# Four modulated convolution layers: two single-bank tiles for the last accumulator, and two steps moved in early iterations

## The chip, the cores and the metric

The kernel runs on one core of a Trainium2 chip. The metric is the time of one execution on the device in microseconds; the median of several executions is compared. The core has a matrix engine (TensorE, PE in the profile, with PEld for its weight loads), a vector engine (VectorE, DVE), a scalar engine (ScalarE, ACT), GpSimd (POOL) and a queue processor (SyncE, SP), which issues most of the DMA transfers. Each works through its own queue in order, and they meet at semaphores. Products land in PSUM, in banks of 512 float32 numbers for each of 128 partitions.

## The reference

`x` is 128 x 64 x 1024 in float32 (samples, channels, positions), `style` 128 x 128.

```python
def _layer(x, style, w, b, mw, mb, typ):
    s = style @ mw.T + mb
    weight = SCALE * w * s[:, None, :, None]
    demod = lax.rsqrt(jnp.sum(weight * weight, axis=(2, 3)) + EPS)
    weight = weight * demod[:, :, None, None]
    if typ == 'same':
        out = jax.vmap(_conv_same)(x, weight) + b[None, :, None]
    elif typ == 'upsample':
        out = jax.vmap(_conv_up)(x, weight.transpose(0, 2, 1, 3)) + b[None, :, None]
        out = _blur(out, 2.0 * blur_k, (1, 1))
    elif typ == 'downsample':
        xb = _blur(x, blur_k, (2, 2))
        out = jax.vmap(_conv_down)(xb, weight) + b[None, :, None]
    return out
...
out = x
for i, typ in enumerate(('same', 'upsample', 'same', 'downsample')):
    out = _layer(out, style, weights[i], biases[i], mod_w[i], mod_b[i], typ)
return x + out
```

Every sample has its own weights of three taps, scaled by its style. There is no nonlinearity between the layers, so for one sample the four layers are one linear map of the signal plus a constant.

## The kernel before, in words

The kernel works on that linear map. For each sample it multiplies the four layers' weights (and the blur) into one filter of nine taps of 64 x 64, and then convolves the signal once with it. The constants that the biases leave in each row, and the few positions at both ends of the signal, are computed apart.

Four samples make a **quad**; there are 32 quads (`NQ`). A quad's work is in two parts.

*Weights.* `scale3` scales layer 3's weights (ScalarE). `stage1` multiplies them by layer 2's into the PSUM tiles psS, and ScalarE evicts them as S. From quad 7 on this is done in two halves: `stage1_a` makes the first products and ScalarE evicts them (line 361); `stage1_b` adds further products to the same banks and VectorE evicts those (line 443). `stage2` multiplies S by the blur and layer 1 (E) into psR, evicted as R, and `stage3` (or `stage3_b` and `stage3_a`) by layer 0 into psW or a free accumulator, evicted as Wf. `combine_a` and `combine_b` (VectorE) form sums H of the nine taps. All PSUM tiles psS, psR and psW come from one pool, `ps_w`, with two tiles of one bank each and one buffer: whoever takes them next waits until the last reader has let go.

*Signal.* The signal lies in three interleaved planes. VectorE and GpSimd make differences of the planes (G and T). The convolution is done in five products instead of nine taps: `conv3`, `conv1`, `conv2`, `conv4` and `conv0`, each of three groups of four matmul instructions, which alternate between two banks: bank s takes the channel rows of half s. `conv3` opens the accumulator psA of the quad; `copy_m3` copies it to SBUF (ScalarE, line 793); `conv1` adds to it; `sum1` forms y (VectorE, line 663); `conv2` adds again; `sum2` forms Y, a second accumulator of two banks that all quads share, and finishes y (line 813); `conv4` adds to Y and `conv0` to psA. `outputs(q, i)` evicts plane i on ScalarE, two banks in turn (`output`, line 831; plane 0 from psA, 1 from y, 2 from Y), and stores each plane. psA comes from the pool `ps_conv`, with two buffers of two banks, each one tile.

The order of the instructions on each engine is the order in which the code is written. One pass of `turn_of(q)` does, mixed with each other, the end of quad q, the signal of n = q + 1, stages 2 and 3 of c = q + 2 and stage 1 of s = q + 4. Iterations 0 to 3 are a variant, `early_turn`; iteration 4 (`entry`) is the first of `turn_of`, with some steps of its own. Behind iteration 28 the last three quads are written out by hand.

Two details matter here. First, in iterations 1 to 6 (`SMALL`) the row constants of the later samples are computed by a pair of small matmuls into spare columns of Y's second bank: VectorE clears these columns with a memset, `small(q)` multiplies into them (line 1238), and VectorE reads them in the next iteration (`small_rest`). Second, waits are found by tile: an instruction that uses a tile waits for the readers or writers of any part of that tile that the framework counts as overlapping, and PSUM accesses of two engines to one tile are put one after another.

Of the kernel before, what the change touches and what calls it, by code (L numbers as in the profile page):

```python
# [55 lines left out]
K = 3  # L56
# [7 lines left out]
def kernel(  # L64
# [12 lines left out]
    NQ = B // 4  # L77
# [20 lines left out]
    ps_w = ctx.enter_context(tc.tile_pool(name="ps_w", bufs=1, space=PSUM))  # L98
# [65 lines left out]
    def unit(pool, name):  # L164

        if pool is ps_w:
            return [pool.tile([P, 512], F32, tag=f"u{r}", name=f"{name}_{r}") for r in range(2)]
        t = pool.tile([P, 2, 512], F32, tag="u", name=name)
        return [t[:, r, :] for r in range(2)]
# [189 lines left out]
    def scaled_copy(eng, dst, src, f):  # L359
        if eng is nc_a:  # L360
            nc_a.activation(dst, src, AF.Copy, scale=f)  # L361
        else:
            eng.tensor_scalar(dst, src, f, None, op0=ALU.mult)
# [23 lines left out]
    def tap_matmul(ps, wd, at, n, weight, taps, first=False, last=False):  # L387
        for r, rows in enumerate(HALF):
            for c, cols in enumerate(HALF):
                nc.tensor.matmul(  # L390
                    ps[r][cols, at * C : (at + n) * C],
                    weight[rows],
                    wd[c if r == 0 else 1 - c][rows, taps],
                    start=first,
                    stop=last,
                    skip_group_check=True,
                )

    def s_tiles(q):
        t = s_pool.tile([P, 2, 8, C], F32, tag="S", name=f"S{q}")  # L400
        return [t[:, r] for r in range(2)], t

    def flat(t):
        return t.rearrange("c a o -> c (a o)")
# [18 lines left out]
    def stage1_a(q, ps=None):  # L423

        ps = ps or unit(ps_w, f"psS{q}")
        wd = chain[q]
        tap_matmul(ps, wd, 2, 2, w2n[:, 0, :], EVEN, first=True)
        tap_matmul(ps, wd, 3, 2, w2n[:, 2, :], EVEN)
        tap_matmul(ps, wd, 1, 1, w2n[:, 1, :], slice(1, 2))
        st, t = s_tiles(q)  # L430
        for r in range(2):
            scaled_copy(nc_a, flat(st[r][:, :4]), ps[r][:, C : 5 * C], tBn[:, q, r : r + 1])
        chain[q] = wd, ps, st, t
# [309 lines left out]
    def product(q, m, ps, groups=range(K)):  # L743

        W, H_ = Wq[q]
        tag, i = SLOT[m]
        for g in groups:
            for s, rows in enumerate(HALF):
                for c, cols in enumerate(HALF):
                    if m in (0, 4):  # L750
                        w = W[rows, tap(m // 2, g), c, :]
                    else:
                        w = H_[rows, m - 1, g, c, :]
                    nc.tensor.matmul(  # L754
                        ps[s][cols, :NB],
                        w,
                        Ts[q, tag][rows, c, i, g : g + NB],
                        start=(g == 0 and m == 3),
                        stop=(g == K - 1),
                        skip_group_check=True,  # L760
                    )

    def m_tile(tag, q, bufs=1):
        return mpool.tile([P, 2, NB], F32, tag=tag, name=f"{tag}_{q}", bufs=bufs)
# [3 lines left out]
    def parts(q):  # L768

        if isinstance(A[q], list):  # L770
            return [(slice(s, s + 1), A[q][s][:, None, :NB]) for s in range(2)]
        return [(slice(0, 2), A[q][:, :, :NB])]

    def banks(q):
        return A[q] if isinstance(A[q], list) else [A[q][:, s] for s in range(2)]
# [3 lines left out]
    def open_a(q):  # L779
        A[q] = ps_conv.tile([P, 2, 512], F32, tag="u", name=f"psA{q}")  # L780
        return banks(q)

    def conv3(q, pool=None):
        if pool:
            A[q] = unit(pool, f"psA{q}")
        elif q not in A:
            open_a(q)
        product(q, 3, banks(q))

    def copy_m3(q):  # L790
        m3c[q] = m_tile("m3", q)
        for s, a in parts(q):
            nc_a.copy(m3c[q][:, s], a)

    def conv1(q, *groups):
        product(q, 1, banks(q), groups or range(K))
# [7 lines left out]
    def conv2(q, *groups):  # L804
        product(q, 2, banks(q), groups or range(K))

    def sum2(q, steps=(0, 1)):
        if 0 in steps:
            m3 = m3c.pop(q)
            for s, a in enumerate(banks(q)):  # L810
                sum_of(Y[:, s, :NB], m3[:, s], 3.0, a[:, :NB])
        for s, a in parts(q) if 1 in steps else ():
            nc_v.tensor_sub(y1w[q][:, s], y1w[q][:, s], a)  # L813

    def conv4(q, *groups):
        product(q, 4, Y_banks, groups or range(K))
# [6 lines left out]
    def output(q, i, s, eng=nc_a):  # L823

        if q not in os:
            os[q] = opool.tile([P, 2, K, NB], F32, tag="o", name=f"o{q}")
        d3, add = td[:, q, s : s + 1], tb[:, q, s : s + 1]
        src = (banks(q)[s][:, :NB], y1w[q][:, s], Y[:, s, :NB])[i]
        dst = os[q][:, s, i]
        if eng is nc_a:  # L830
            nc_a.activation(dst, src, AF.Identity, bias=add, scale=d3)  # L831
        else:
            eng.tensor_scalar(dst, src, d3, add, op0=ALU.mult, op1=ALU.add)

    def store(q, s, planes=slice(0, K), queue=nc.sync):
        queue.dma_start(
            out[q, :, s, planes.start * NB : planes.stop * NB],
            os[q][:, s, planes].rearrange("c i j -> c (i j)"),
        )
# [11 lines left out]
    def last(i, n, j):  # L851
        ps, w = ends_ps[0]
        return ps[i][:, : n * w].rearrange("c (b j) -> c b j", b=n)[:, :, :j]
# [105 lines left out]
    def spread(t, n):  # L959

        return t[:, :, None].to_broadcast([P, t.shape[1], n])
# [132 lines left out]
    def rest3():  # L1094
        for h in range(2):
            bs = slice(h * HB, (h + 1) * HB)
            nc_v.scalar_tensor_tensor(
                Oe[:, bs],
                last(h, HB, 3),
                0.125,  # L1100
                spread(dm[:, 3, bs], 3),
                op0=ALU.mult,
                op1=ALU.mult,
            )
# [204 lines left out]
    def late(q):  # L1309
        return AHEAD <= q < NQ - 2  # L1310

    def outputs(q, i):
        for r in range(2):
            output(q, i, r)
            if late(q):
                store(q, r, slice(i, i + 1))
# [96 lines left out]
    def turn_of(q):  # L1413
        n, c, s = q + 1, q + 2, q + 4
        entry = q == FIRST
        stage2(c)
        if entry:
            sum2(q)
            conv4(q)
            combine_a(n)  # L1420
            r_sums(c, nc_v)
        else:
            conv2(q)
            r_sums(c, nc_g)
            sum2(q)
            in2(n, nc_g)
        side(TABLES, q)
        for i in range(3):
            load(c + 1, slice(i, i + 1))
        stage3_b(c, open_a(n))  # L1430
        if entry:
            conv0(q, 0, 1)
        else:
            combine_a(n)
            conv4(q)
        stage3_a(c)
        combine_b(n)
        conv3(n)
        if entry:
            copy_m3(n)  # L1440
        outputs(q, 2)
        if s < NQ:
            stage1_a(s)
        if not entry:
            copy_m3(n)
        in04(n)
        if sharing(q):
            share_sums(c + 1)
        in_g2(c)
        side(SIDE, q)  # L1450
        if q in SMALL:
            l, bs = SMALL[q]
            nc_v.memset(high(bs.stop - bs.start), 0.0)
        conv0(q, *((2,) if entry else range(K)))
        if entry:
            conv1(n, 0, 1)
        outputs(q, 1)
        if s < NQ:
            stage1_b(s)
        in_g01(c)  # L1460
        if sharing(q):
            share(c + 1, banks(q))
            share_copy(c + 1)
        outputs(q, 0)
        if q in SLOTS:
            matmuls, width, rest = SLOTS[q]
            slot(matmuls, width, Y_banks)
            rest()
        if s == NQ:
            slot(ends3, 3, unit(ps_w, "psE"), 3)  # L1470
            rest3()
        if q in SMALL:
            small(q)
        conv1(n, *((2,) if entry else range(K)))
        sum1(n)
        in3(c)
        side(LATE, q)
        if s == NQ:
            in04(c)
        in1(c, nc_g)  # L1480
        if s + 1 < NQ:
            scale3(s + 1)
# [6 lines left out]
    q, n, c = NQ - 3, NQ - 2, NQ - 1  # L1489
# [30 lines left out]
    in2(c, nc_v)  # L1520

    q, n = NQ - 2, NQ - 1
    conv3(n)
    copy_m3(n)
    conv4(q, 0, 1)
    for i in range(2):
# [109 lines left out]
```

## Time and profile before

| what | value |
|---|---|
| median of three runs | 479.57 us (479.07 to 479.76) |
| profiled execution: time / span | 480.28 us / 478.5 us |
| TensorE busy | 470.0 us, 98% |
| VectorE busy | 417.8 us, 87% |
| ScalarE busy | 310.1 us, 65% |
| GpSimd busy | 162.6 us, 34% |
| moved by DMA | 70.70 MB, 148 GB/s on the mean |
| granted TensorE clock | 0.997 |

The span runs from the first to the last instruction of the profiled execution; its time has 1.8 us more around it. In a row of the timeline the first number is the start, the second the length of a merged group, then engine, line, operation, tiles (out<-in), the shape and the count; in brackets stands the idle time of the engine ahead of it and what ended it. A row of a weight load (PEld) shows best where TensorE had to wait.

### The profile page before, as it was taken

The numbers are of one execution on the slowest core, as the hardware profiler recorded it, in microseconds if no ns is written. First come the engines' busy times: TensorE is split into PE (matmuls) and PEld (weight loads), VectorE is DVE, ScalarE is ACT, GpSimd is POOL, SyncE is SP. The second block draws the span as 40 slices with busy tenths as digits, with TensorE's granted clock in tenths as the row PEclk, the third lists the DMA queues.
The fourth block names the chain that finished last, engine by engine and source line by source line (L and its number), as shares of the span: only waits on it lengthen the run. The fifth ranks groups of instructions, "written<-read, shape, count | busy, mean of one in ns | idle before, by whom it ended". The sixth has DMA issues, their size and how long they took to land.

```text
span 478.5 us, 26719 instructions
## 1 busy us (share of the span) xinstructions
PE 470.0 (98%) x11928; PEld 348.4 (73%) x11928; DVE 417.8 (87%) x689; ACT 310.1 (65%) x708; POOL 162.6 (34%) x197
## 2 busy tenths in 40 slices
PE   8999999999999999999999999999999999999995
PEld 7877797777778876677776677767898777766652
DVE  5789998879889899899979899979989999999895
ACT  5465657577766676766667666667666767766352
POOL 2434033664435342243432233422333432333200
PEclk9999999999999999999999999999999999999998
DMA  7115356444455554355553455534555554445125
GB/s 234 58 68 182 130 184 204 149 121 154 147 150 150 180 156 144 121 150 159 171 160 118 123 170 152 179 122 126 144 164 166 165 149 148 149 146 174 61 91 191
DMA packets 50514, 70.70 MB, mean 148 GB/s; under 512 B 5664, under 2 KB 47328, under 8 KB 50400
## 3 DMA queue, kind: packets, MB, share of 16 engines
q1 hardware_dynamic: 49808, 68.32, 45.8%
q8 instruction: 93, 1.52, 1.5%
q10 hardware_dynamic: 592, 0.69, 0.5%
q14 instruction: 21, 0.17, 0.1%
HBM read 35.36 MB, written 33.62 MB: 144 GB/s over the span
## 4 chain that ended last, share of the span: by engine, by line
PE 95%; DVE 2%; DMA 1%; issue 0%; ACT 0%; SPq 0%; ACTq 0%
PE psA L754 45%; PE Y L754 11%; PE psR L468 9%; PE psA L572 7%; PE psW L572 7%; PE psS L390 6%; PE psR L534 4%; PE psA L468 2%; PE Y L995 2%; DMA par_s<-in_params_s 1%; DVE H L663 1%; PE Y L337 1%; DVE G L663 0%; PE psM L205 0%; ACT o L831 0%
## 5 line engine op out<-in xcount | busy, mean ns | idle before, releaser
L754 PE MATMUL psA<-T,H 64*64 64x340 f32 x2304 | 186.6, 447 | 0.4 <-DVE y L663 0.2
L754 PEld LDWEIGHTS psA<-T,H 64*64 64x64 f32 x2304 | 90.9, 133 | 48.1 <-issue 2.6
L663 DVE SCALAR_TENSOR_TENSOR G<-X 128x1376 f32<-128x1376 f32 (+2 forms) x65 | 78.0, 1206 | 0.6 <-DMA X<-in_x 0.4
L727 POOL TENSOR_TENSOR T<-G 128x684 f32<-128x684 f32 x28 | 46.5, 1661 | 73.7 <-DVE G L663 71.1
L446 POOL TENSOR_TENSOR S<-S 128x128 f32<-128x128 f32 x28 | 21.2, 756 | 143.7 <-ACT S L361 136.3
L361 ACT ACTIVATE R<-psR,tC 128x448 f32<-128x448 f32 x63 | 36.5, 630 | 45.8 <-PE psR L468 26.2
L754 PE MATMUL psA<-T,Wf 64*64 64x340 f32 x768 | 63.9, 446 | 0.0
L754 PE MATMUL Y<-T,Wf 64*64 64x340 f32 x768 | 62.8, 451 | 0.1
L663 DVE SCALAR_TENSOR_TENSOR Y<-m,psA 128x340 f32<-128x340 f32 x64 | 33.1, 517 | 28.5 <-PE psA L754 27.1
L361 ACT ACTIVATE psW<-psA 128x128 f32<-128x128 f32 x100 | 19.3, 269 | 49.9 <-PE psA L572 45.8
L741 DVE TENSOR_TENSOR T<-G 128x1368 f32<-128x1368 f32 (+1 forms) x33 | 50.7, 1540 | 0.0
L361 ACT ACTIVATE Wf<-psW,t 128x256 f32<-128x256 f32 (+2 forms) x76 | 32.7, 479 | 26.7 <-PE psW L572 26.4
L712 DVE TENSOR_TENSOR T<-X 128x684 f32<-128x684 f32 x32 | 47.5, 1486 | 0.0
L468 PE MATMUL psR<-S,E 64*64 64x64 f32 (+1 forms) x1472 | 46.9, 237 | 0.0
L732 POOL TENSOR_TENSOR T<-G 128x684 f32<-128x684 f32 x28 | 46.5, 1660 | 0.0
L390 PEld LDWEIGHTS psS<-wd,w2n 64*64 64x64 f32 x1120 | 35.0, 133 | 13.3 <-ACT S L361 0.8
L468 PEld LDWEIGHTS psR<-S,E 64*64 64x64 f32 x1472 | 40.4, 134 | 4.9 <-ACT psR L491 0.2
L754 PEld LDWEIGHTS Y<-T,Wf 64*64 64x64 f32 x768 | 29.7, 132 | 17.7 <-DVE Y L663 0.7
L831 ACT ACTIVATE o<-psA,tb,td 128x340 f32<-128x340 f32 x63 | 37.1, 647 | 6.3 <-PE psA L754 6.3
L754 PEld LDWEIGHTS psA<-T,Wf 64*64 64x64 f32 x768 | 29.1, 133 | 15.1
L831 ACT ACTIVATE o<-Y,tb,td 128x340 f32<-128x340 f32 x63 | 36.6, 638 | 4.5 <-PE Y L754 2.7
L831 ACT ACTIVATE o<-y,tb,td 128x340 f32<-128x340 f32 x62 | 38.5, 678 | 0.6 <-DVE y L813 0.6
(164 smaller groups left out, 834.3 us busy)
## 6 DMA issues: line engine op xcount, KB each, us to landing
out<-o SPq DMA_DIRECT2D x167, 170.0 KB, 2.6
X<-in_x SPq DMA_DIRECT2D x150, 172.0 KB, 3.3
X<-in_x SPq DMA_DIRECT2D x14, 516.0 KB, 5.6
out<-o SPq DMA_DIRECT2D x6, 510.0 KB, 5.6
out<-o SPq DMA_DIRECT2D x2, 340.0 KB, 2.7
Xe<-in_x_ends SPq DMA_DIRECT2D x1, 512.0 KB, 6.7
out<-o ACTq DMA_DIRECT2D x3, 170.0 KB, 2.3
par<-in_params SPq DMA_DIRECT2D x2, 192.0 KB, 3.5
```

Source lines behind the costliest of these rows:

```text
L361: nc_a.activation(dst, src, AF.Copy, scale=f)
L390: nc.tensor.matmul(ps[r][cols, at * C : (at + n) * C], weight[rows], wd[c if r == 0 else 1 - c][rows, taps], start=first, stop=last, skip_ ...
L446: nc_g.tensor_add(t[:, :, 2], t[:, :, 2], t[:, :, 0])
L468: nc.tensor.matmul(dst[r][cols], weight[rows], st[c if r == 0 else 1 - c][rows, slots, :], start=False, stop=last, skip_group_check=True,)
L572: nc.tensor.matmul(dst[r][cols], weight[rows], t[rows, c, slots, :], start=first, stop=last, skip_group_check=True,)
L663: nc_v.scalar_tensor_tensor(out, x, f, y, op0=ALU.mult, op1=op)
L712: nc_v.tensor_sub(t[:, pairs, 0, :NJ], plane(X, 3, pairs), plane(X, 1, pairs))
L727: eng.tensor_add(t[:, :, 0, :NJ], plane(g, 2), plane(g, 1))
L732: eng.tensor_sub(t[:, :, 1, :NJ], plane(g, 2), plane(g, 1))
L741: nc_v.tensor_sub(t[:, pairs, :, :NJ], both(a, PL), both(b, 1))
L754: nc.tensor.matmul(ps[s][cols, :NB], w, Ts[q, tag][rows, c, i, g : g + NB], start=(g == 0 and m == 3), stop=(g == K - 1), skip_group_check ...
L831: nc_a.activation(dst, src, AF.Identity, bias=add, scale=d3)
```

## The change

Three edits. In iteration 4 the first half of stage 1 for quad 8, with ScalarE's two evictions of S8, is issued before plane 2 of quad 4 is evicted (two ScalarE evictions of Y and their stores); in the other iterations the order stays. In `turn_of` the row constants' two matmuls come behind `conv1` (iterations 4, 5 and 6). And the last quad's accumulator is two tiles of one bank each, out of `ps_w`, where it was one tile of two banks out of `ps_conv`; `copy_m3`, `sum1` and the second step of `sum2` run over the parts that they find (`parts`), so for this quad each becomes two instructions of 340 columns where it was one of 680.

```diff
@@ turn_of
         conv3(n)
         if entry:
             copy_m3(n)
+            stage1_a(s)
         outputs(q, 2)
-        if s < NQ:
-            stage1_a(s)
         if not entry:
+            if s < NQ:
+                stage1_a(s)
             copy_m3(n)
         in04(n)
@@ turn_of
         if s == NQ:
             slot(ends3, 3, unit(ps_w, "psE"), 3)
             rest3()
+        conv1(n, *((2,) if entry else range(K)))
         if q in SMALL:
             small(q)
-        conv1(n, *((2,) if entry else range(K)))
         sum1(n)
@@ the last quads
     q, n = NQ - 2, NQ - 1
-    conv3(n)
+    conv3(n, ps_w)
     copy_m3(n)
     conv4(q, 0, 1)
```

What the last line leads to:

```python
def parts(q):
    if isinstance(A[q], list):
        return [(slice(s, s + 1), A[q][s][:, None, :NB]) for s in range(2)]
    return [(slice(0, 2), A[q][:, :, :NB])]
...
def conv3(q, pool=None):
    if pool:
        A[q] = unit(pool, f"psA{q}")
```

## The prediction

> **What bounds the kernel now.** I read the page first: the busy times and the chain of work that ended last, then the busy time of each engine by stretch, then the timeline at the three places that the diff touches, and last the landing times of single stores.
>
> ```profile
> span 478.5 us, 26719 instructions
> ...
> PE 470.0 (98%) x11928; PEld 348.4 (73%) x11928; DVE 417.8 (87%) x689; ACT 310.1 (65%) x708; POOL 162.6 (34%) x197
> ...
> PE 95%; DVE 2%; DMA 1%; issue 0%; ACT 0%; SPq 0%; ACTq 0%
> ...
> L663 DVE SCALAR_TENSOR_TENSOR Y<-m,psA 128x340 f32<-128x340 f32 x64 | 33.1, 517 | 28.5 <-PE psA L754 27.1
> ```
>
> ```profile
> 103.00:450.00 347.00, 346.66 (x9337) 255.60 (x9332) 311.85 (x482) 234.84 (x550) 122.53 (x116) 1.00 0.50 151
> ```
>
> TensorE carries 95% of the chain. Between 103 and 450 us it is busy 346.66 of 347.00 us, so nothing in that stretch can be won except work, and none is removed. VectorE is at 311.85 of 347.00 there, and once in each iteration it sits waiting for TensorE's product before it makes Y: 27.1 us over 32 quads, 0.85 us a quad. So a TensorE that arrives some tenths of a microsecond earlier is not at once held by VectorE. What can be won lies where TensorE stands still: before 103 us, and in the last 28 us. The diff touches both.
>
> **Iteration 4: S8's two evictions ahead of the two of Y.** These rows are the timeline from 98 to 104 us.
>
> ```profile
> 98.61 0.73 PE L390 MATMUL psS<-wd,w2n 64*64 64x128 f32 x24
> ...
> 98.86 0.72 ACT L793 COPY m<-psA 128x680 f32<-128x680 f32 x1 [0.95 <-PE psA L754]
> ...
> 99.48 1.17 ACT L831 ACTIVATE o<-Y,tb,td 128x340 f32<-128x340 f32 x2
> ...
> 99.74 1.32 PE L754 MATMUL psA<-T,H 64*64 64x340 f32 x16
> 100.15 3.75 SPq L836 DMA_DIRECT2D out<-o  x6
> 100.53 0.85 ACT L361 ACTIVATE S<-psS,tBn 128x256 f32<-128x256 f32 x2
> 100.74 0.14 DVE L1453 MEMSET Y<- 128x96 f32 x1 [1.64 <-ACT o L831]
> 101.06 0.20 PEld L390 LDWEIGHTS psS<-wd,w2n 64*64 64x64 f32 x4 [0.60 <-ACT S L361]
> ...
> 101.24 1.25 ACT L831 ACTIVATE o<-y,tb,td 128x340 f32<-128x340 f32 x2
> 101.43 0.25 PEld L390 LDWEIGHTS psS<-wd,w2n 64*64 64x64 f32 x10 [0.17 <-ACT S L361]
> ...
> 101.92 0.61 DVE L443 SCALAR_TENSOR_TENSOR S<-psS,tB,S 128x128 f32<-128x128 f32 x2 [1.04 <-ACT o L831]
> 102.33 2.40 PEld L534 LDWEIGHTS psR<-S,E 64*64 64x64 f32 x67 [0.35 <-DVE S L443]
> ...
> 104.06 1.66 SPq L146 DMA_DIRECT2D X<-in_x  x2
> ```
>
> ScalarE goes m3, Y, Y, S8, S8, y, y without a gap. TensorE's second half of stage 1 must wait until S8 is out of psS8: 0.60 us for the first bank and 0.17 us for the second. Stage 2 of quad 7 then waits 0.35 us more, because its two accumulators take psS8's banks, which VectorE's S8 evictions (101.92) set free.
>
> Swapped, S8 starts at 99.48; psS8's first half ended at 98.61 + 0.73 = 99.34, so it is ready. The S8 pair ends at 99.48 + 0.85 = 100.33, a microsecond sooner, and both waits of TensorE go. The Y pair starts where the step from S8 to the next puts it (101.24 - 100.53 = 0.71 later): 100.19, and ends at 101.36. The y pair keeps its 101.24.
>
> What is late next is the memset of Y's spare columns on VectorE. It waits for ScalarE's reads of Y and began 100.74 - (99.48 + 1.17) = 0.09 after them, so it moves from 100.74 to 101.45. Behind it in VectorE's queue stand the S8 evictions on which stage 2 waits, and TensorE's row-constant matmuls wait for it too. In iteration 5 (rows below) an S eviction starts 0.05 us after the memset, so here at 101.50 instead of 101.92: 0.42 us sooner. Stage 2's 102.33 becomes 101.91. TensorE is by then just through with the rest: product 1's first two thirds are 1.32 us from 99.74, behind them come 0.25 us of stage 1, the last third (half of 1.32, as matmuls overlap a little less) and the constants, which makes 101.9 to 102.1. **Gain 0.42 us.** Bounds: if none of the ScalarE steps overlapped (99.48 + 0.85 + 1.17 + 0.09 + 0.05 + some 0.25 of lost overlap = 101.9) nothing is gained, and 0.60 + 0.17 = 0.77 is all that TensorE waits for S8. The stores of Y's planes leave 0.71 us later; those behind them in SP's queue, and the load at 104.06, follow the last eviction of iteration 4, which keeps its time, so the move costs nothing there.
>
> **Row constants behind the first product.** In iteration 4 this only lets four product instructions go before the late memset. In iteration 5:
>
> ```profile
> 114.88 0.45 PEld L468 LDWEIGHTS psA<-S,E 64*64 64x64 f32 x24
> ...
> 115.25 0.14 DVE L1453 MEMSET Y<- 128x96 f32 x1
> ...
> 115.30 0.55 DVE L443 SCALAR_TENSOR_TENSOR S<-psS,tB,S 128x128 f32<-128x128 f32 x2
> 115.44 0.14 PEld L1238 LDWEIGHTS Y<-cc,wsum 64*64 64x64 f32 x2
> ```
>
> The weight loads of the step before end at 115.33; the constants' load comes at 115.44, after the memset's end at 115.39. The product behind them needs nothing of it. Ahead of them it starts **0.11 us** sooner, and the constants, 1.7 us later, find the memset long done. Their reader is VectorE in the next iteration, so nobody waits. In iteration 6 the constants do not wait, and two equal pieces of TensorE work change places: 0. Bounds for both: 0 to 0.2.
>
> So TensorE is 0.53 us earlier from 116 us on, and by the stretch row it keeps that to 450 us.
>
> **The last quad.** Its accumulator's two banks were one tile; now each is followed by itself. The three handovers of 680 columns become two of 340 each.
>
> ```profile
> 462.79 0.72 ACT L793 COPY m<-psA 128x680 f32<-128x680 f32 x1 [2.54 <-PE psA L754]
> ...
> 463.57 1.39 PEld L754 LDWEIGHTS psA<-T,H 64*64 64x64 f32 x24 [0.33 <-ACT m L793]
> ...
> 465.68 0.87 DVE L663 SCALAR_TENSOR_TENSOR y<-psA,m 128x680 f32<-128x680 f32 x1 [0.31 <-PE psA L754]
> ...
> 466.60 1.35 PEld L754 LDWEIGHTS psA<-T,H 64*64 64x64 f32 x24 [0.50 <-DVE y L663]
> ...
> 468.02 0.60 DVE L1109 SCALAR_TENSOR_TENSOR Oe<-Oe,par_s,Xe 64x384 f32<-64x384 f32 x1
> ...
> 468.68 1.07 DVE L663 SCALAR_TENSOR_TENSOR Y<-m,psA 128x340 f32<-128x340 f32 x2
> ...
> 469.80 1.35 PEld L754 LDWEIGHTS Y<-T,Wf 64*64 64x64 f32 x24 [0.71 <-DVE Y L663]
> ...
> 473.76 0.63 ACT L831 ACTIVATE o<-psA,tb,td 128x340 f32<-128x340 f32 x1 [1.09 <-PE psA L754]
> 474.43 0.34 ACTq L836 DMA_DIRECT2D out<-o  x1
> 474.43 0.63 DVE L833 TENSOR_SCALAR o<-psA,td,tb 128x340 f32<-128x340 f32 x1 [1.09 <-ACT o L831]
> 475.09 0.33 SPq L836 DMA_DIRECT2D out<-o  x1
> ```
>
> The split work costs more in sum. y in halves is two of 517 ns (the Y row of the page has that form) for one of 0.87; overlapped by the 0.1 us that neighbours show, the second bank is done 0.04 us later and the first 0.3 us sooner. The copy of m3 in halves I take as even: the first can start when its own bank is done. So the product after y starts early on one bank and 0.04 us late on the other. The next handover, Y, was waiting for both banks; its first half now needs one, and VectorE is free for it at 468.02 + 0.60 = 468.62 instead of 468.68. I take **0.08 us** for it, which passes through product 4 at 469.80 to the end. Bounds: a loss of 0.2, if the halves do not overlap (2 x 0.517 + 0.03 against 0.87), and a gain of 0.1.
>
> The larger piece is the end. VectorE's last eviction waits 1.09 us, and ends that wait behind ScalarE's eviction of the other bank, since both read one tile. As built, it now waits for TensorE instead. It moves from 474.43 to 473.77, beside ScalarE's, and the last store is issued at 474.43 instead of 475.09: 0.66 us. The two last stores then leave together, so I look at landing times: first the only two stores issued together, at 471.4, then the last one from ScalarE and the last one from SP.
>
> ```profile
> out<-o SPq DMA_DIRECT2D x1, 170.0 KB, 2.8
> out<-o ACTq DMA_DIRECT2D x1, 170.0 KB, 3.1
> ```
>
> ```profile
> out<-o ACTq DMA_DIRECT2D x1, 170.0 KB, 2.1
> ```
>
> ```profile
> out<-o SPq DMA_DIRECT2D x1, 170.0 KB, 2.5
> ```
>
> The last lands at 475.09 + 2.5 = 477.6. Issued at 474.43, alone it would land 0.66 sooner; by the pair's 3.1 it would land at 477.53 and gain nothing. But the pair at 471.4 had another store issued half a microsecond ahead of it, which these two will not have. The second of the pair landed 0.3 us behind the first. With a lone store's 2.1 to 2.5 for the first here, the later one lands 2.4 to 2.8 after 474.43; against 477.6 that is 0.3 to 0.7. I take **0.47**, a little below the middle because of the pair's own rows.
>
> The Trainium skill ("DMA: Bandwidth & Descriptors", section "Issuing engines are not separate DMA queues") speaks against this part: transfers issued by different engines run on the same 16 DMA engines and interleave, so issuing from two saves only the issue time. By it the whole would be 0.61 instead of 1.08; the pair's 2.8 and 3.1 against 2.1 and 2.5 go its way, though by less than a whole transfer.
>
> **Sum.** 0.42 + 0.11 + 0.08 + 0.47 = 1.08 us. The profiled execution took 480.28 us (span 478.5 and 1.8 around it) and would take 479.20. It lies 0.71 above the median of the three runs, 479.57 (479.07 to 479.76), and the difference is what I carry over: **478.5 us**, 0.23% less.
>
> **The rivals.** *The last stores are not slowed by each other*: 0.66 instead of 0.47, 1.27 us in all, 478.3. For it: the 2.1 and 2.5 of lone stores. *They are slowed fully*, to the pair's 3.1, since they share the engines that move them: 0.61 in all, 479.0. Against it: the store ahead of that pair. *The early gain is not kept*: 0.55 remains from the end, 479.0. For it would speak a stop of TensorE in mid-kernel; the stretch row has 0.34 us in 347. *Slower*: the shift of 0.53 us changes which VectorE and GpSimd instructions run side by side in the steady iterations, and VectorE, at 90% there, becomes the last to arrive. It decides once a quad loses the 0.85 us that VectorE now waits for TensorE; then 0.1 us for each of 23 iterations is 2.3 us, less the 1.08: 480.8. Break-even is 0.05 us a quad. Against it: VectorE's and GpSimd's steps are released by the same TensorE work and shift with it.
>
> **How the numbers follow.** 0.2% (0.96 us) is about what a measurement of this kernel can tell from no change. Forecast 0.50 (478.1 to 478.9 by its own terms; 0.7 of it beyond 0.2%), unhindered stores 0.22 (all of it), full contention 0.12 and early gain lost 0.08 (both within 0.2%), slower 0.08. So faster 0.57, same 0.35, slower 0.08. The range takes in both 479.0 cases with the lower bounds of the handovers, and the unhindered one: 477.9 to 479.35.
>
> **What would show it.** Right: TensorE's load of psS's second half in iteration 4 without its 0.60 and 0.17 us; stage 2 of quad 7 at 101.9; the memset at 101.45; iteration 5's first product directly behind the shared sums; the end of TensorE 0.6 us earlier; the last two evictions side by side, and the last two stores issued within 0.05 us. Wrong: a wait of stage 2 for VectorE's S8 at 102.3 or later, idle time of TensorE for VectorE or GpSimd between 117 and 450 us, a handover of the last quad that ends over 0.2 us later, or a last store that lands 3.1 us after its issue.

## The result and the profile after

The changed kernel takes 478.20 us (median of 12 executions, 476.68 to 479.25) where the kernel before takes 479.66 on the same chip (12 executions, 479.07 to 480.72): ratio 0.9969, 95% interval 0.9960 to 0.9978, or 1.49 us less (1.06 to 1.92). Forecast were 478.5 us and 1.08 us less. The profiled execution took 478.26 us (span 476.5), 2.02 us less than the profiled one of before.

The page of the changed kernel first: the span, the busy times, the engines' shares of the chain, and VectorE's wait for TensorE before Y.

```profile
span 476.5 us, 26723 instructions
...
PE 469.4 (99%) x11928; PEld 354.6 (74%) x11928; DVE 417.6 (88%) x691; ACT 310.2 (65%) x709; POOL 164.0 (34%) x197
...
PE 95%; DVE 3%; DMA 1%; issue 0%; ACT 0%; SPq 0%; ACTq 0%; DVEq 0%
...
L663 DVE SCALAR_TENSOR_TENSOR Y<-m,psA 128x340 f32<-128x340 f32 x64 | 33.1, 516 | 27.9 <-PE psA L754 26.7
```

TensorE still carries 95% of the chain, and the wait before Y is as long as it was (26.7 us against 27.1), so the rival *slower*, in which VectorE arrives last in the steady iterations, did not come about. The same stretch by engine (length, then busy time and instructions of PE, PEld, DVE, ACT, POOL, then granted clock, DMA share and GB/s):

```profile
103.00:450.00 347.00, 347.00 (x9371) 258.92 (x9366) 313.01 (x485) 235.18 (x550) 123.41 (x116) 1.00 0.50 151
```

TensorE's 346.66 us of before have become 347.00. The third of a microsecond that it stood still before, and what it was, comes up again below; no edit touches it.

Iteration 4, in the timeline of the changed kernel:

```profile
99.46 0.84 ACT L361 ACTIVATE S<-psS,tBn 128x256 f32<-128x256 f32 x2
...
100.18 1.17 ACT L831 ACTIVATE o<-Y,tb,td 128x340 f32<-128x340 f32 x2
...
100.58 0.56 PEld L390 LDWEIGHTS psS<-wd,w2n 64*64 64x64 f32 x16
...
101.04 0.21 PEld L754 LDWEIGHTS psA<-T,H 64*64 64x64 f32 x8
...
101.45 0.14 DVE L1454 MEMSET Y<- 128x96 f32 x1 [2.37 <-ACT o L831]
101.50 0.53 DVE L443 SCALAR_TENSOR_TENSOR S<-psS,tB,S 128x128 f32<-128x128 f32 x2
101.70 0.22 PEld L1238 LDWEIGHTS Y<-c0f,wsum 64*64 64x64 f32 x4 [0.45 <-issue]
...
101.84 2.61 PEld L534 LDWEIGHTS psR<-S,E 64*64 64x64 f32 x72
```

ScalarE takes S8 at 99.46, then Y. TensorE's second half of stage 1 (100.58) has no wait left. The memset stands at 101.45 and VectorE's S8 evictions at 101.50, both as forecast, and stage 2 starts at 101.84 where 101.91 was forecast. The two profiles may be compared by the clock here: up to iteration 4 they differ by 0.02 us.

Iteration 5:

```profile
114.38 0.45 PEld L468 LDWEIGHTS psA<-S,E 64*64 64x64 f32 x24
...
114.73 1.36 PEld L754 LDWEIGHTS psA<-T,H 64*64 64x64 f32 x24
114.74 0.14 DVE L1454 MEMSET Y<- 128x96 f32 x1
...
114.79 0.55 DVE L443 SCALAR_TENSOR_TENSOR S<-psS,tB,S 128x128 f32<-128x128 f32 x2
...
116.22 0.42 PEld L1238 LDWEIGHTS Y<-cc,wsum 64*64 64x64 f32 x4
```

The product follows the shared sums directly (114.73), and the constants come 1.34 us after the memset's end, without a wait.

The last quad, from two stretches of the timeline:

```profile
464.07 0.93 DVE L663 SCALAR_TENSOR_TENSOR y<-psA,m 128x340 f32<-128x340 f32 x2 [0.28 <-PE psA L754]
...
464.63 1.76 PEld L754 LDWEIGHTS psA<-T,H 64*64 64x64 f32 x24
...
467.00 1.12 DVE L663 SCALAR_TENSOR_TENSOR Y<-m,psA 128x340 f32<-128x340 f32 x2
...
468.17 0.78 PEld L754 LDWEIGHTS Y<-T,Wf 64*64 64x64 f32 x16 [0.64 <-DVE Y L663]
...
471.70 0.34 ACTq L836 DMA_DIRECT2D out<-o  x1
...
471.93 0.63 DVE L833 TENSOR_SCALAR o<-psA,td,tb 128x340 f32<-128x340 f32 x1 [0.26 <-PE psA L754]
472.09 0.63 ACT L831 ACTIVATE o<-psA,tb,td 128x340 f32<-128x340 f32 x1 [1.09 <-PE psA L754]
472.75 0.34 ACTq L836 DMA_DIRECT2D out<-o  x1
```

The last two evictions lie side by side, and the wait of VectorE for ScalarE (1.09 us before) is gone. VectorE's is released by TensorE. ScalarE's starts 0.05 us after its own queue has issued the store ahead of it (471.70 + 0.34 = 472.04), so there the bracket, which doesn't count the issue as work, names the wrong one. SP's store leaves at 472.59, ScalarE's at 472.75. Their landings, from the DMA issues of the two stretches around them (last number: us from issue to landing):

```profile
out<-o SPq DMA_DIRECT2D x1, 170.0 KB, 2.5
```

```profile
out<-o ACTq DMA_DIRECT2D x1, 170.0 KB, 2.8
```

So the last to be issued, now ScalarE's, lands 2.8 us after its issue, the later end of the 2.4 to 2.8 of the forecast.

For the rest I cut every profile into the same segments. The first weight load of `conv4` (Y<-T,Wf) marks each iteration; the start goes to the first mark, the tail from the mark of iteration 29 to TensorE's last product, and the landing from there to the last landing. All in us:

| kernel | start | it. 0-3 | it. 4 | it. 5 | it. 6-28 | tail | landing | span |
|---|---|---|---|---|---|---|---|---|
| before | 32.02 | 59.64 | 16.53 | 14.21 | 328.72 | 22.35 | 4.09 | 478.5 |
| after | 32.02 | 59.62 | 16.04 | 14.01 | 327.80 | 22.35 | 3.70 | 476.5 |

The 2.02 us are 0.49 in iteration 4, 0.20 in iteration 5, 0.92 in iterations 6 to 28, and 0.39 in the last landing. The change touches nothing that should shorten the 0.92.

### The profile page after: what moved, and what is told of

Its sections match the earlier page's. It is cut to its first block, busy times and chain, and to the rows that moved or that the text cites. A ratio compares the mean times of both kernels' runs of the same rounds, so it can differ in the third digit from the quotient of the medians.

```text
span 476.5 us, 26723 instructions
## 1 busy us (share of the span) xinstructions
PE 469.4 (99%) x11928; PEld 354.6 (74%) x11928; DVE 417.6 (88%) x691; ACT 310.2 (65%) x709; POOL 164.0 (34%) x197
## 4 chain that ended last, share of the span: by engine, by line
PE 95%; DVE 3%; DMA 1%; issue 0%; ACT 0%; SPq 0%; ACTq 0%; DVEq 0%
PE psA L754 45%; PE Y L754 11%; PE psR L468 9%; PE psA L572 7%; PE psW L572 7%; PE psS L390 6%; PE psR L534 4%; PE psA L468 2%; PE Y L995 2%; PE Y L337 1%; DMA par_s<-in_params_s 1%; DVE H L663 1%; DVE G L663 0%; PE psM L205 0%; DVE Y L663 0%; DVE y L813 0%
## 5 line engine op out<-in xcount | busy, mean ns | idle before, releaser
L754 PE MATMUL psA<-T,H 64*64 64x340 f32 x2304 | 186.4, 447 | 0.3 <-DVE y L663 0.2
L754 PEld LDWEIGHTS psA<-T,H 64*64 64x64 f32 x2304 | 92.9, 133 | 45.5 <-issue 2.3
L754 PE MATMUL psA<-T,Wf 64*64 64x340 f32 x768 | 64.2, 446 | 0.0
L754 PE MATMUL Y<-T,Wf 64*64 64x340 f32 x768 | 62.8, 451 | 0.0
L663 DVE SCALAR_TENSOR_TENSOR Y<-m,psA 128x340 f32<-128x340 f32 x64 | 33.1, 516 | 27.9 <-PE psA L754 26.7
L361 ACT ACTIVATE Wf<-psW,t 128x256 f32<-128x256 f32 (+2 forms) x76 | 32.7, 480 | 26.7 <-PE psW L572 26.4
L754 PEld LDWEIGHTS Y<-T,Wf 64*64 64x64 f32 x768 | 30.7, 132 | 16.7 <-DVE Y L663 0.6
L754 PEld LDWEIGHTS psA<-T,Wf 64*64 64x64 f32 x768 | 30.8, 133 | 13.4
```

The source lines that it names most:

```text
L663: nc_v.scalar_tensor_tensor(out, x, f, y, op0=ALU.mult, op1=op)
L754: nc.tensor.matmul(ps[s][cols, :NB], w, Ts[q, tag][rows, c, i, g : g + NB], start=(g == 0 and m == 3), stop=(g == K - 1), skip_group_check ...
```

## The experiments

Theory A: each edit acts at its own place, and the rest of the difference is chance. Theory B, the rival: a TensorE that arrives earlier also loses fewer of its short standstills in mid-kernel. Lines with + and - in the diffs are against the kernel before unless it is said otherwise.

### One edit at a time

*s8_only* is the move of S8's evictions alone.

```diff
         if entry:
             copy_m3(n)
+            stage1_a(s)
         outputs(q, 2)
-        if s < NQ:
-            stage1_a(s)
```

> Only S8's evictions ahead of the two of Y in iteration 4; constants and last quad as before. Theory A (each edit acts at its own place, and the rest of the measured gain of 1.5 us is chance standstills of TensorE in mid-kernel): 0.35 to 0.5 us less than before; the constants' matmuls stand ahead of the last third of product 1 and wait for the late memset (101.45), so up to 0.15 us of the 0.51 may be missing at stage 2 of quad 7. Theory B (an earlier TensorE also loses fewer of the 0.3 us standstills in stage 3 of the steady iterations): 0.9 to 1.3 us less.

*const_only* is the move of the row constants alone.

```diff
+        conv1(n, *((2,) if entry else range(K)))
         if q in SMALL:
             small(q)
-        conv1(n, *((2,) if entry else range(K)))
```

> Only the row constants behind product 1 in iterations 4 to 6. Theory A: 0.1 to 0.2 us less than before, all of it in iteration 5 (115.30 to 117). Theory B: 0.4 to 0.9 us less, since the standstills after 140 us go as well.

*last_only* is the last quad's accumulator alone.

```diff
-    conv3(n)
+    conv3(n, ps_w)
```

> Only the last quad's accumulator in two single-bank tiles. Theory A and B: nothing moves ahead of 460 us; the last two evictions run side by side, and the time falls by 0.4 to 0.5 us (0.39 at the last landing and 0.06 in the handovers of the changed kernel's trace). A third reading, that the last stores hold each other up fully: 0 to 0.1 us.

*s8_last* has S8's move and the last quad, without the constants' move.

> The changed kernel without the constants' move. Theory A: 0.8 to 0.95 us less than before, 0.15 to 0.3 us more than the changed kernel. Theory B: within 0.1 us of the changed kernel if the S8 swap alone is shift enough to lose the standstills.

| kernel | start | it. 0-3 | it. 4 | it. 5 | it. 6-28 | tail | landing | span | ratio to before (95%) |
|---|---|---|---|---|---|---|---|---|---|
| s8_only | 31.71 | 59.72 | 16.46 | 14.15 | 328.25 | 22.35 | 3.85 | 477.4 | 1.0003 (0.9987 to 1.0018) |
| const_only | 33.03 | 59.65 | 16.53 | 14.01 | 327.68 | 22.35 | 3.92 | 478.1 | 1.0011 (0.9995 to 1.0027) |
| last_only | 32.14 | 59.60 | 16.53 | 14.88 | 328.19 | 22.35 | 3.37 | 478.0 | 0.9984 (0.9966 to 1.0001) |
| s8_last | 33.30 | 59.73 | 16.46 | 14.20 | 327.91 | 22.35 | 3.42 | 478.3 | 0.9993 (0.9979 to 1.0008) |

By time none of these can be told from no change. The segments tell more. S8's move alone gains 0.07 us in iteration 4, not 0.42; the constants' move alone nothing there; the two together 0.49. The last quad alone brings the landing from about 4 us to 3.4, and nothing to the tail. So A's expectation is borne out for the constants (0.20 us), and missed for S8's move, alone (0.07 us for 0.35 to 0.5) and with the last quad (some 0.6 for 0.8 to 0.95). The last quad alone gains some 0.6 at the landing, for 0.4 to 0.5. The timeline of s8_only shows where the 0.42 went:

```profile
101.25 0.14 DVE L1454 MEMSET Y<- 128x96 f32 x1 [2.35 <-ACT o L831]
...
101.50 0.19 PEld L1238 LDWEIGHTS Y<-c0f,wsum 64*64 64x64 f32 x3 [0.57 <-issue]
101.54 0.30 PE L1238 MATMUL Y<-c0f,wsum 64*64 64x96 f32 x2 [0.47 <-DVE Y L1454]
...
101.90 2.22 PEld L534 LDWEIGHTS psR<-S,E 64*64 64x64 f32 x58
```

With the constants ahead of the product, TensorE meets them at about 100.94 and stands 0.57 us, until the memset has gone through, which S8's move made 0.7 us later. The last third of the product and stage 2 stand behind them.

### Is it the memset?

*s8_clear* is s8_only with the memset of iteration 4 issued at that iteration's start, where VectorE stands free; *after_clear* is the changed kernel with the same addition.

```diff
+        # at the start of iteration 4
+            l, bs = SMALL[q]
+            nc_v.memset(high(bs.stop - bs.start), 0.0)
...
-        if q in SMALL:
+        if q in SMALL and not entry:   # the memset's old place
```

> S8's evictions ahead, row constants left ahead of the first product, and the memset of iteration 4 moved to that iteration's start. Theory 1 (the swap alone gained only 0.07 us because the row constants' matmuls stand ahead of the product and wait for the memset, which the swap makes 0.7 us later): with the memset early the gain of the swap comes without moving the constants, iteration 4 takes 16.0 to 16.1 us instead of 16.46. Theory 2 (what is missing is on ScalarE or in psS8's banks): iteration 4 stays at 16.4 to 16.5.

> The changed kernel, with iteration 4's memset of Y's spare columns moved to the start of the iteration, where VectorE stands free, so that nothing waits for ScalarE's late reads any more. If the late memset (101.45) still holds VectorE's evictions of S8, these start when psS8 is done and stage 2 comes earlier by up to the 0.07 us that separate it from TensorE's own work: iteration 4 takes 15.95 to 16.04 us. If the memset that is early costs the iteration's own first steps, up to 0.14 us (its length) later: 16.18. Either way the whole kernel stays within 0.2 us of the changed kernel (ratio to the kernel before 0.997 to 0.998).

s8_clear: iteration 4 takes 16.29 us, between the two theories (its profiled time, 480.80 us, has 1.7 us of standstills in iterations 0 to 3 and in iteration 5, of the kind described below). Its timeline:

```profile
101.63 0.61 DVE L443 SCALAR_TENSOR_TENSOR S<-psS,tB,S 128x128 f32<-128x128 f32 x2 [2.31 <-ACT o L831]
101.72 0.19 PEld L1238 LDWEIGHTS Y<-c0f,wsum 64*64 64x64 f32 x3 [0.34 <-issue]
101.75 0.30 PE L1238 MATMUL Y<-c0f,wsum 64*64 64x96 f32 x2 [0.23 <-ACT o L831]
```

With the memset out of the way the constants still wait 0.34 us, now for ScalarE's reads of Y, ended at 101.60: they write into the same tile. So of the 0.42 us that the constants' place cost, 0.17 go with the memset (16.46 to 16.29), and 0.25 remain while the constants wait for ScalarE. With the constants behind the product, as in the change, both are gone (16.04).

after_clear: iteration 4 takes 16.08 us against 16.04, ratio to before 0.9977 (0.9962 to 0.9991), 478.28 us. VectorE's S8 evictions do start 0.11 us sooner after the iteration's mark, but nothing is gained, so in the changed kernel the memset is not what ends last. This is no better version.

### What ends the last landing?

*one_evictor* is the changed kernel with both of the last evictions on ScalarE.

```diff
-    for i, (eng, queue) in enumerate(zip(BOTH, (nc_a, nc.sync))):
+    for i, (eng, queue) in enumerate(zip((nc_a, nc_a), (nc_a, nc.sync))):
```

> The changed kernel, with both of the last quad's final evictions on ScalarE, one behind the other, and the two stores on their two queues as before. Theory 1 (what the end gains is that the second eviction no longer stands behind the first): the last store is issued 0.5 to 0.7 us later and the last landing comes 3.9 to 4.1 us after TensorE's end instead of 3.4 to 3.7. Theory 2 (the two stores limit each other, whenever they are issued): the landing stays at 3.4 to 3.7.

```profile
472.68 0.63 ACT L831 ACTIVATE o<-psA,tb,td 128x340 f32<-128x340 f32 x1 [1.08 <-PE psA L754]
473.34 0.34 ACTq L836 DMA_DIRECT2D out<-o  x1
473.73 0.63 ACT L831 ACTIVATE o<-psA,tb,td 128x340 f32<-128x340 f32 x1 [0.42 <-ACT o L831]
```

One behind the other, with ScalarE's own store between them, the second eviction starts 1.05 us after the first, and the last landing comes 4.18 us after TensorE's end, a little beyond the 3.9 to 4.1 of theory 1 and far from theory 2: what the end gains is that the evictions go side by side.

### Both kernels again, and the change without the last quad

> The changed kernel once more, unaltered, to see what two profiles of one program differ by. Theory A (every edit acts at its own place; the rest of the difference between profiles is chance): iteration 4 again 16.04 us, iteration 5 again 14.01, the end of TensorE's tail again 22.35 and the last landing 3.4 to 3.7 after it, each within 0.1; but the start before the first product (31.7 to 33.3 so far) and the steady iterations (327.7 to 328.7) differ from the first profile by some tenths, because TensorE's standstills of 0.3 us in mid-kernel fall differently. Theory B (a TensorE that is 0.7 us earlier loses fewer standstills): the steady iterations are again 327.8 within 0.1, without a standstill. Against the kernel before: A 1.1 us faster (ratio 0.9977), B 1.5 to 2.0 (0.9958 to 0.9969).

> The kernel before once more, unaltered, for a second profile. Theory A: iteration 4 again 16.53 us, iteration 5 14.2, TensorE's tail 22.35, landing 3.85 to 4.1 after it; the start and the steady iterations differ from the first profile by some tenths. Theory B: the steady iterations are again at 328.7, with the standstills of 0.30 us at the same places.

*s8_const* has S8's and the constants' move, and the last quad as it was.

> Edits 2 and 3 without the last quad's two tiles. Theory A (each edit at its own place, the rest chance): iteration 4 takes 16.04 us, iteration 5 14.01, TensorE's tail 22.35, and the last landing 3.85 to 4.1 us after TensorE's end, as in the kernel before. Sum 0.49 + 0.20 = 0.69 us less than before, ratio 0.9986. Theory B (the earlier TensorE also loses 0.5 to 1 us of standstills in mid-kernel): ratio 0.9965 to 0.9975.

| kernel | start | it. 0-3 | it. 4 | it. 5 | it. 6-28 | tail | landing | span | ratio to before (95%) |
|---|---|---|---|---|---|---|---|---|---|
| after_again | 32.37 | 59.74 | 16.04 | 14.01 | 328.15 | 22.31 | 3.48 | 477.0 | 0.9978 (0.9964 to 0.9992) |
| before_again | 31.32 | 59.65 | 16.53 | 14.95 | 328.47 | 22.35 | 4.13 | 478.3 | one execution, 480.12 us |
| s8_const | 31.51 | 59.71 | 16.05 | 14.01 | 327.86 | 22.35 | 3.91 | 476.3 | 0.9979 (0.9964 to 0.9995) |

Iteration 4, the tail, and iteration 5 with the constants moved repeat within 0.06 us; the start and iterations 6 to 28 do not (328.15 us, where B had needed 327.8 again). The landing spreads more: without the split accumulator it takes 3.85 to 4.13 us (before, before_again, s8_only, const_only, s8_const, and 3.97 in s8_clear), with it 3.37 to 3.70 (after, after_again, last_only, s8_last, after_clear 3.63, and 3.43 in pad128, a run of the next part). The changed kernel's second comparison gives 1.06 us less (0.38 to 1.73), close to A's 1.1, though 1.5 lies inside it. s8_const's ratio lies between what A and B expected and its interval holds both, so the times don't separate them.

### What the standstills hang on

The second profile of before speaks against B's picture of fixed places: its standstills lie at 122.44, 380.32 and 394.37 us, while the first had its own at 150.43, 339.00 and 353.13, 0.30 us each. One row of each, from the timelines of weight loads; first before:

```profile
150.43 0.13 PEld L572 LDWEIGHTS psA<-R,w0s 64*64 64x64 f32 x1 [0.30 <-issue]
```

and before_again:

```profile
122.44 0.13 PEld L572 LDWEIGHTS psA<-R,par 64*64 64x64 f32 x1 [0.84 <-issue]
```

"issue" says that nothing in the profile released them. I numbered all of TensorE's records (weight loads, matmuls and the 130 of its sequencer) in order of time, from 0: these six have the numbers 7105, 17345, 18113, 5569, 19649 and 20417, and each leaves a remainder of 193 when divided by 256. *pad64* and *pad128* put 64 and 128 more records early into the changed kernel.

```diff
     zeros_to_y(2, 96, False)
+    zeros_to_y(8, 16, False)      # pad128: zeros_to_y(16, 16, False)
```

> The changed kernel with 16 more weight loads and matmuls per quarter, 64 records of TensorE in all, early in the start-up, where TensorE waits for parameters; they multiply zeros into spare columns. It is to show what TensorE's standstills hang on, which no releaser explains. Theory I (they come every 256 records of TensorE's own stream, where the next block of its instructions is fetched): each of them comes 64 records earlier in the program, about 1.2 us, so the one in the 150s near 148.8 instead of 150.0, the one in the 190s near 191.8 instead of 193.0, and the row of regular 0.13 us gaps near 196.9, 210.7 and 224.5 instead of 198.1, 211.9 and 225.8 (all less the difference of the two starts). Theory P (they belong to a place in stage 3 or to a neighbour's access there): same places in the program, within 0.1 us of the first product of their iteration.

> As the run with 64 more records, with 128. Theory I: all standstills come 128 records earlier, about 2.4 us, so near 147.6, 190.6, 195.7, 209.5 and 223.4 (less the difference of the two starts). Theory P: same places as without.

pad64: span 476.7 us, iterations 6 to 28 328.24 us, landing 4.63; pad128: 477.5, 329.36 and 3.43. I take the waits of at least 0.15 us ahead of a weight load, between 104 and 452 us, that exceed the median of all 14 profiles at the same instruction by over 0.06 and lie outside the steps that the edits move. There are 30 at records with that remainder of 193, one of 0.15 us two records ahead of one of them, and two at a fixed place, in the two kernels with the early memset. In pad64 the one standstill (0.26 us, 202.98) and in pad128 all six have the remainder 193 in their own count, and so lie 64 and 128 records earlier in the program, six of the seven in the convolution's products (L754) where all others were in stage 3 (L572). At record 9409, near 193 us, the weight load comes 0.02 to 0.45 us late in all twelve profiles of unshifted count, and not late at all in pad64 and pad128. So the count decides, not the place. My expectation was wrong in its detail: no standstill came back "1.2 us earlier" one by one, and the row of 0.13 us gaps that I had put among them stayed where it was, since it belongs to the program.

The count has a partner, the queue of instructions on the page of the changed kernel (transfers, MB, share of the DMA engines):

```profile
q8 instruction: 93, 1.52, 1.5%
```

93 transfers of 16 KB for 23,986 records of TensorE is one for 258 records; pad128 has 94. Among the DMA queues of before in the stretch from 147.4 to 149 us lies one of them:

```profile
q8 instruction: 1, 0.02, 5.1%
```

It ended at 148.87 us, and TensorE went on at 150.43, 1.56 us later. In all 14 profiles, between 110 and 450 us, 34 waits of at least 0.15 us lie at such a count, and every one ends 1.24 to 1.56 us after the last such transfer's end; among all 1,008 passages of such a count only one comes sooner after one. So I read the standstills as TensorE waiting for its next block of instructions: the count says where, and the transfer's end says when they end. How often that happens differs from one execution to the next; that a transfer is slowed by the data that the same DMA engines move would fit (they took 0.9 to 2.0 us each), but no run varied that.

That leaves B as a matter of chance rather than of the change: iterations 6 to 28 took 327.80 to 328.34 us in the five profiles with both early edits and unshifted count, and 327.68 to 328.72 in the seven without. The means, 328.07 and 328.25, are no further apart than the scatter. One observation stays open: the standstill at about 123 us (0.77 to 0.87 us, in iteration 5) was in three profiles (before_again, last_only, s8_clear), with 0.16 us in a fourth (s8_last), all with the constants at their old place, and in none where they were moved. If that is more than chance, it adds to the change's gain; four of six profiles against none of eight, at a place picked because it stood out, is too little to say so.

## Why the prediction was right, and where its steps were not

The parts, in us:

| step | forecast | measured | how |
|---|---|---|---|
| S8's evictions ahead, iteration 4 | 0.42 | 0.07 alone, 0.49 with the constants' move | 16.53 to 16.46, and to 16.04 |
| constants, iteration 5 | 0.11 | 0.20 | 14.21 to 14.01 |
| last quad's handovers | 0.08 | 0.00 | 22.35 in both |
| last evictions and stores | 0.47 | 0.47 | means of six landings each, 3.98 and 3.51 |
| sum | 1.08 | 1.16 | |

The sum of the places that the change touches, 1.16 us, lies within the measured interval of both comparisons (1.06 to 1.92 and 0.38 to 1.73). The rest of the profiles' 2.02 us is, to within 0.1 us, the standstills: three of 0.30 us fell into iterations 6 to 28 of the profile before and none into the one after.

**The step that failed is the constants' price in iteration 4.** The prediction wrote that there the move "only lets four product instructions go before the late memset", and counted 0. It had itself noted that TensorE's row-constant matmuls wait for the memset, and that S8's move puts it at 101.45. But it then took 0.42 us from the release of stage 2 by VectorE's S8 evictions alone, as if the constants in TensorE's queue were not in front. They were: without their move S8's is worth 0.07 (s8_only, s8_last). The two edits' total was right because it added up TensorE's work in the new order, in which the constants come last, and so counted the gain of two edits as that of one. Steps forecast for that order, the memset at 101.45 and S8 at 101.50, came to the hundredth.

**Iteration 5** was sized too small. The 0.11 us were counted from the end of the shared sums' weight loads (115.33), but the next load doesn't wait for that end: in the changed kernel the product's first starts at 114.73, 0.10 us before the shared sums' last has ended (114.38 + 0.45 = 114.83). So the product starts 0.35 us after the shared sums' first load, where it was 0.56 to the constants' load before. The value lies at the edge of its bounds, 0 to 0.2.

**The handovers** gained nothing. The first half of y does go to TensorE sooner: the product behind it waited 0.50 us before and has 0.11 now. But its instructions alternate between the banks, so it soon stands on the second half, and that comes 0.08 us later than the one step of 680 columns did (15.51 against 15.43 us after the iteration's mark). VectorE's first half of Y starts 0.05 us sooner (17.51 against 17.57), as predicted in kind. Its second half, on which product 4 waits, starts at the same 18.12 us. It doesn't wait for its bank: TensorE's last matmul into that had ended at 17.50, by the profile. But it needs two things now, the first half of Y and TensorE's bank, and the first of these waits stands in VectorE's queue as an instruction of its own (18.05 to 18.07). That fits its start, 0.10 us after the first half's end, where it was 0.03 us with the one wait of before. TensorE's wait shrinks from 0.71 to 0.64 us only because another quad's product ahead of it ends 0.07 us later, and its end doesn't move. The prediction let the 0.06 us that the first half of Y gains pass to the end; they pass only if the second half is early too.

**The end.** The evictions go side by side as said. That the landing gains just the 0.47 us of the forecast is in part luck, since two misses cancel. The forecast put VectorE's eviction beside ScalarE's, 0.66 us sooner. It comes 0.87 us sooner (0.96 us after TensorE's end before, 0.10 after the change), and ScalarE's starts behind it, held by its own store issue. The last store is now ScalarE's: it is issued 0.71 us sooner than the last one was (0.92 us after TensorE's end against 1.63), and takes 0.24 us longer to land (2.59 us against 2.35, means of the same six profiles each). The forecast's own 2.4 to 2.8 us also give 0.36 to 0.76 us, where it wrote 0.3 to 0.7. By the Trainium skill ("DMA: Bandwidth & Descriptors", section "Issuing engines are not separate DMA queues") transfers issued by different engines interleave on the same 16 DMA engines, and two issuers save only the issue time. The trace agrees in that the stores do slow each other, by those 0.24 us; that nothing would be gained here, as the prediction worked out from it, did not come about. The one profile that goes that way is pad64, where the last six stores were issued within 1.8 us instead of 3.0, the last three took 3.6 to 3.7 us each, and the last landing came 4.63 us after TensorE's end; it isn't in the means above, and with it the mean of the split kernels would be 3.67.

**The rivals.** *Unhindered* stores would have shown 0.66, *fully slowed* ones 0; neither came. *The early gain is not kept*: it was kept: the stretch row has TensorE busy 347.00 of 347.00 us, and the profiles with both early edits pass iterations 6 to 28 no slower than those without (328.07 and 328.25 us on the mean). *Slower*: VectorE's wait before Y stayed at 0.83 us a quad.

## What to carry to other kernels

Before you price a step by the wait that it removes, walk through the queue of the engine that waits: an instruction that stands ahead there, and depends on what the move makes later, takes the gain, and then two edits are worth something only together. Splitting a tile by banks brings something where two engines read the halves side by side at the end of the program, and nothing where the next product alternates between the halves and needs the later one anyway, which the split can even make later. For differences of a microsecond compare segments of repeated profiles, each around one edit, ahead of spans: here the segments around the edits repeated within 0.06 us while the spans of the changed kernel's two profiles differed by half a microsecond, and its twelve executions ran from 476.68 to 479.25 us.

## What the runs showed of the hardware

TensorE can stand still at every 256th of its records, for up to 0.9 us in mid-kernel, until 1.2 to 1.6 us have passed since the last 16 KB transfer on the instruction queue; the profile lists this as "issue" or, worse, under another engine's name, as this row of pad128 does, whose record count is 21,953 (remainder 193) and which came 1.37 us after such a transfer's end:

```profile
419.11 0.78 PEld L754 LDWEIGHTS psA<-T,H 64*64 64x64 f32 x16 [0.29 <-POOL T L727]
```

The same wait sits in the start-up at record 449, near 14 us: in eight of the twelve profiles without added records TensorE's weight loads stand there for 0.35 to 2.0 us. The start as a whole took 31.3 to 33.3 us in the twelve, and 30.88 and 31.81 with the added records; the two longest starts (const_only and s8_last) have another cause that was not looked for further.

At the end of the program VectorE began its eviction 0.10 us after the end of TensorE's last product, as the profile models that end, in both profiles of the changed kernel. ScalarE's 0.25 us there says nothing of its answer to TensorE, since its own queue was issuing a store until 0.05 us before.
